# Residual additions of two attention blocks: four of nine by adding transfers, five on VectorE

## The chip, the cores and the metric

The kernel runs on one core of a Trainium2 chip. The metric is the device time of one execution in microseconds (us). Before the change it is 3370.97 us, the median of three runs (3370.32 to 3372.03). The profile is of one more execution, with a span of 3364.5 us from the first to the last instruction.

The engines are TensorE (PE in the profile, with its weight loads as PEld), VectorE (DVE), ScalarE (ACT), GpSimd (POOL) and SyncE (SP, which here only issues transfers). Each runs its own instructions in order and waits on semaphores for the others.

## The reference

The input x has 8 images of 512 channels and 32 x 32 points, in float32. Two attention blocks follow one another:

```python
def block(x, gn_w, gn_b, wq, wk, wv, bq, bk, bv, wp, bp):   # for each of two layers
    xn  = group_norm(x, 8 groups, eps=1e-5) * gn_w + gn_b     # over channels and points
    q, k, v = wq @ xn + bq, wk @ xn + bk, wv @ xn + bv        # 512 x 512 by 512 x 1024
    o   = softmax(q.T k / 8) v                                # 8 heads of 64, 1024 tokens
    return x + wp @ o + bp                                    # the residual addition
x = block(block(x, layer 0), layer 1)
```

Eight images times two layers are 16 jobs, taken in pairs of images: (image 0, layer 0), (1, 0), (0, 1), (1, 1), (2, 0) and so on. The change concerns the last line of the block, the addition of the projected output to x.

## The kernel before

Each job has three parts: a v phase, a deep phase and the attention. The v phase forms V by seven products of halves (Winograd's form of a 2 x 2 block product). The deep phase of job n forms the output O of job n - 1 and then K and Q of job n. Each of the three is again split into seven products of halves, called chains here, and each chain is split once more into seven products of 128 x 128 by 128 x 256. So the deep phase has 21 chains (O: 0 to 6, K: 7 to 13, Q: 14 to 20) with 147 products.

The products of two neighbouring chains alternate on TensorE. A chain works on four PSUM banks z, y, u, w in this order, ScalarE and VectorE taking the results out:

```python
ORDER = (1, 5, 6, 2, 7, 3, 4)            # the seven products of a chain
OUTER = (1, 2, 6, 5, 7, 3, 4)            # the seven chains of O, of K, of Q
def step(o):                             # bank that product o writes or adds into
    product(o, {1: z, 5: w, 6: z, 2: y, 7: z, 3: u, 4: z}[o], o in (1, 5))
    if o == 1:   nc.scalar.copy(y, z)
    elif o == 5: put5(w)                 # ScalarE copies w to s5
    elif o == 6: nc.scalar.copy(u, z)
    elif o == 2: put(0, 0, y)            # ScalarE: quarter of p
    elif o == 7: put(1, 1, z)            # VectorE: z + s5 into a quarter of p
    elif o == 3: put(0, 1, u)            # VectorE: u + s5
    else:        put(1, 0, z)            # ScalarE
```

The four quarters make one tile p of 128 x 1024 for each chain. All p tiles come from one pool of six buffers, so chain c writes the buffer that chain c - 6 had:

```python
LEAD = 2
epool = ctx.enter_context(tc.tile_pool(name="epool", bufs=LEAD + 4))
...
e = epool.tile([P, 2, HALF], F32, tag="e", name=f"p_{n}_{c}")
```

A p tile of O is then added into one or two quarters of x. The quarter is named by (output half, token half), and the additions are transfers, issued by GpSimd, that add to what they find:

```python
def more(oh, sh, part, ends=False):
    cols = slice(sh * HALF, (sh + 1) * HALF)
    to_ = xt[:, 2 * oh : 2 * oh + 2, cols]
    nc.gpsimd.dma_start(to_, p(part), accum_op=ALU.add)
    if ends and layer == 1:               # the last addition into this quarter
        ... later(8.0, lambda: nc.sync.dma_start(out[...], to_))

if o == 1:   more(0, 0, 1)
elif o == 2: more(0, 0, 2, True)
elif o == 6:
    add(p(6), p(6), p(1))                 # VectorE, 128 x 1024
    outer.append(lambda: more(0, 1, 6))
elif o == 5:
    more(1, 1, 5)
    outer.append(lambda: more(0, 1, 5))
elif o == 7:
    add(p(7), p(7), p(6))
    outer.append(lambda: (more(1, 1, 7, True), more(1, 0, 7)))
elif o == 3: more(0, 1, 3, True)
elif o == 4: more(1, 0, 4, True)
```

VectorE's larger work in the deep phase waits in lists, from which one piece is taken after the puts of products 7 and 3 of each chain:

```python
if ORDER[j] in (7, 3):
    if soon:  soon.popleft()()            # sums of O's inputs that a later chain needs
    if outer: outer.popleft()()           # additions of p tiles
    elif extra and extra[0][0] <= c:      # the rest: sums for K, statistics of x, ...
        extra.popleft()[1]()
```

What is left of `extra` is done in the following attention. There the normed input xn of the next job is made by ScalarE, at attention steps 22, 24, 26 and 28, with a factor mul and an offset off that VectorE computes at step 20. An attention has 64 steps.

The output bias (wp @ bv + bp) is computed once per layer from rows of wp: `multiply` forms the product with bv in place, and `add_up` sums it, for each of four row blocks.

Of the kernel before, what the change touches and what calls it, by code (L numbers as in the profile page):

```python
# [12 lines left out]
ALU = mybir.AluOpType  # L13
AX = mybir.AxisListType
# [4 lines left out]
P = 128  # L19
# [7 lines left out]
NC = C // P  # L27
# [9 lines left out]
CH = C // 2  # L37
# [33 lines left out]
def fast_path(  # L71
# [10 lines left out]
    nc = tc.nc  # L82
# [10 lines left out]
    out_bias = acts.tile([P, 2, NC], F32, name="out_bias")  # L93
# [12 lines left out]
    def later(delay, fn):  # L106
        todo.append((clock[0] + delay, fn))
# [93 lines left out]
    def used(key):  # L201
        del held[key]
        later(2.5, fetch)
# [296 lines left out]

            return [first, lambda: self.pair[1]()]

    def deep_phases(n, extra, outs=None):

# [5 lines left out]
        def job(which):  # L512
            return n - 1 if which == O else n
# [71 lines left out]
        def end(c):  # L585
            which, o = chains[c]
            m = job(which)
            used((m, which, o))

            def p(k):  # L590
                return tiles[which, k]

            def add(to_, a, b):
                outer.append(lambda: nc.vector.tensor_add(to_, a, b))  # L594

            if which == O:
                b, layer = jobs[m]
                xt = xs[b]

                def more(oh, sh, part, ends=False):  # L600

                    cols = slice(sh * HALF, (sh + 1) * HALF)
                    to_ = xt[:, 2 * oh : 2 * oh + 2, cols]
                    nc.gpsimd.dma_start(to_, p(part), accum_op=ALU.add)  # L604
                    if ends and layer == 1:
                        rows = slice(oh * CH, (oh + 1) * CH)
                        later(8.0, lambda: nc.sync.dma_start(
                            out[b, rows, cols].rearrange("(c p) s -> p c s", p=P), to_
                        ))

                if o == 1:
                    more(0, 0, 1)
                elif o == 2:
                    more(0, 0, 2, True)
                elif o == 6:
                    add(p(6), p(6), p(1))
                    outer.append(lambda: more(0, 1, 6))
                elif o == 5:
                    more(1, 1, 5)
                    outer.append(lambda: more(0, 1, 5))  # L620
                elif o == 7:
                    add(p(7), p(7), p(6))
                    outer.append(lambda: (more(1, 1, 7, True), more(1, 0, 7)))
                elif o == 3:
                    more(0, 1, 3, True)
                elif o == 4:
                    more(1, 0, 4, True)
                return
            d = dst[which]

            def quarter(oh, sh):
                return d[:, 2 * oh : 2 * oh + 2, sh * HALF : (sh + 1) * HALF]

            if o == 2:
                add(quarter(0, 0), p(1), p(2))
            elif o == 6:
                add(p(6), p(6), p(1))
            elif o == 5:
                add(quarter(0, 1), p(6), p(5))
            elif o == 7:  # L640
                add(p(7), p(7), p(6))
                add(quarter(1, 1), p(7), p(5))
            elif o == 3:
                add(quarter(0, 1), quarter(0, 1), p(3))
            elif o == 4:
                add(quarter(1, 0), p(7), p(4))

        live = {}
        soon, outer = deque(), deque()

        def thunk(c, j):
            def go():
# [21 lines left out]
        at = sorted((7 * c + 2 * j, c, j) for c in range(len(chains)) for j in range(7))  # L674
        return [thunk(c, j) for _, c, j in at]

    def plain_weights(n):
        layer = jobs[n][1]
        w = acts.tile([P, NC, C], F32, tag="deep", name="w_last")
        nc.sync.dma_start(w, wp[layer].rearrange("(cc p) o -> p cc o", p=P))  # L680
        return w
# [231 lines left out]
    def make_out_bias(layer):  # L913

        rows, bvb = [], []

        def load():
            bvb.append(apool.tile([P, C], F32, tag="px", name=f"bvb_{layer}"))
            nc.sync.dma_start(bvb[0], bv[layer : layer + 1, :].to_broadcast([P, C]))
            for i in range(2):  # L920
                rows.append(apool.tile([P, 2, HALF], F32, tag="acc", name=f"rows_{layer}_{i}"))
                nc.sync.dma_start(
                    rows[i],
                    wrows[layer][i * CH : (i + 1) * CH].rearrange("(oc p) c -> p oc c", p=P),
                )

        def multiply(oc):
            r = rows[oc // 2][:, oc % 2, :]
            nc.vector.tensor_mul(r, r, bvb[0])

        def add_up(oc):
            r = rows[oc // 2][:, oc % 2, :]
            nc.vector.tensor_reduce(out_bias[:, layer, oc : oc + 1], r, AX.X, ALU.add)
            if oc == NC - 1:
                a0 = layer * NVEC + BP
                nc.vector.tensor_add(
                    out_bias[:, layer, :], out_bias[:, layer, :], env.vec_sb[:, a0 : a0 + NC]
                )
                nc.vector.tensor_sub(
                    out_step[:, layer, :], out_bias[:, layer, 0:2], out_bias[:, layer, 2:4]  # L940
                )

        steps = [lambda oc=oc, fn=fn: fn(oc) for oc in range(NC) for fn in (multiply, add_up)]
        return load, steps

    def first_factors(put, which_layers):

# [128 lines left out]
    extra = deque((0, lambda part=part: factor(q0, part)) for part in range(4))  # L1076
    extra.append((1, lambda: store_factors(q0, 0, Q)))
    load, bias_steps = make_out_bias(0)
    extra.append((2, load))
    extra.extend((5, fn) for fn in bias_steps)  # L1080
    reads, steps = norm_steps(1)
    extra.extend((9, fn) for fn in reads)
    for n in range(-1, len(jobs)):
        last = n + 1 == len(jobs)
        outs = None
        if n >= 0:
            chores = {}

            def put(i, fn):
                while i in chores:  # L1090
                    i += 1
                chores[i] = fn

            if last:
                w = plain_weights(n)
            else:
                if n == 0:
                    first_factors(put, [(O, 0), (V, 1)])
                elif n == 1:
                    first_factors(put, [(K, 1), (Q, 1)])  # L1100
                elif n == 2:
                    first_factors(put, [(O, 1)])
                for i, (_, fn) in enumerate(extra):
                    put(2 + i, fn)
                at = (10, 20, 22, 24, 26, 28, 36, 39, 42, 45)
                for i, fn in zip(at, steps + sums(n + 1)):
                    put(i, fn)
                deep_first = deep_steps(n + 1)
                for at, fn in zip((52, 54, 57, 59), deep_first[4:]):
                    put(at, fn)  # L1110
                put(61, lambda: (extend_plan(n + 1), [fetch() for _ in range(RING)]))
            assert max(chores, default=0) < NT * len(att.groups)
            att.run(chores)
            banks(0, "one")
            banks(1, "one")
            if last:
                advance(100.0)
                advance(100.0)
                judge()
                plain_proj(n, w)  # L1120
                break
            outs = OutputSums(n)
            out_sums(n, outs)
            first = v_phase(n + 1, ORDER)
            for thunk in first[:-1]:
                thunk()
            rest = first[-1:]
            extra = deque((0, fn) for fn in deep_first[:4])
            if jobs[n][1] == 1 and jobs[n][0] + 2 < B:
                extra.append((11, lambda b=jobs[n][0] + 2: (x_tile(b), load_x(b))))  # L1130
            if n == 1:
                load, bias_steps = make_out_bias(1)
                extra.append((8, load))
                extra.extend((11, fn) for fn in bias_steps)
            if n + 2 < len(jobs):
                reads, steps = norm_steps(n + 2)
                extra.extend((15, fn) for fn in reads)
        both = deep_phases(n + 1, extra, outs)
        both[0]()
        rest[0]()  # L1140
        if n < 0:
            later(12.0, lambda: load_x(1))
        for thunk in both[1:-3]:
            thunk()
        banks(0, "two")
        att = Attention(n + 1)
        att.scores(0)
        att.scores(1)
        for thunk in both[-3:]:
            thunk()  # L1150
        banks(1, "two")
# [249 lines left out]
```

## Time and profile before

| What | Value |
|---|---|
| time, median of three runs | 3370.97 us |
| span of the profiled execution | 3364.5 us, mean granted PE clock 0.989 |
| adding transfers x<-p | 135 of 512 KB, median 8.5 us from issue to landing |
| their queue (q0) | 12.2% of 16 engines' span |
| all other transfers of the kernel (q1) | 25.0% |

Times in the profile are in microseconds from the start of the span; means of one instruction are in nanoseconds. L565 is line 565 of the kernel. Names of tiles are the program's, without numbers: `zd` is the bank z of a chain of the deep phase, `p` its tile, `x<-p` an adding transfer. In a timeline, the figures are start, duration, engine, line, operation, output and inputs, and the number of instructions merged. What stands in brackets is the time that the engine was idle before it and what ended it. TensorE executes each product of the deep phase as two records, so a row with x2 is one product. A wait for several semaphores is put down to the one that came last.

Of the lines that form the parts: L565 is a product of the deep phase, L434 of the v phase, L723 and L754 of the attention. L575 and L577 are ScalarE's puts into p, L579 and L581 VectorE's, L381 is the copy of z to y, L385 that of z to u, L594 an addition of p tiles on VectorE, and L604 the issue of an adding transfer.

### The profile page before, as it was taken

How to read it: one execution, taken by the hardware profiler on the slowest of the kernel's cores; microseconds unless marked ns; L12 is line 12 of the kernel's file. 1: busy time of each engine (PE TensorE's matmuls, PEld its weight loads, DVE VectorE, ACT ScalarE, POOL GpSimd, SP SyncE). 2: the span in 40 equal slices, each digit the busy share in tenths (PEclk: the TensorE clock that was granted, in tenths of full speed). 3: DMA queues.
4: the chain of work that ended last, by engine and by line, in shares of the span. 5: the costliest groups of instructions: out<-in, count | busy, mean ns of one | idle time of the engine just before them, and what ended most of it. 6: DMA issues, size and time to landing. Idle time of an engine off the chain costs nothing. (4 is left out here: it accounts for less than half of the span.)

```text
span 3364.5 us, 57800 instructions
## 1 busy us (share of the span) xinstructions
PE 3248.1 (97%) x22870; PEld 1872.5 (56%) x22870; DVE 2701.4 (80%) x3895; ACT 1889.1 (56%) x3022; POOL 189.3 (6%) x166
## 2 busy tenths in 40 slices
PE   9999989999999999999999999999999999999999
PEld 7365473663746638365473654736547365573743
DVE  8996978969689696886968879687796877968776
ACT  4645646456465564655646556564655646556463
POOL 0000010000100001000010000101001010010100
PEclk9999999999999999999999999999999999999999
DMA  8235271360713407135180431605417052160611
GB/s 303 92 113 135 73 222 66 99 179 21 219 33 87 120 21 181 27 99 153 30 225 24 113 89 37 174 18 132 126 42 216 15 151 57 48 160 15 164 59 40
DMA packets 169320, 351.32 MB, mean 104 GB/s; under 512 B 35033, under 2 KB 47953, under 8 KB 168017
## 3 DMA queue, kind: packets, MB, share of 16 engines
q1 hardware_dynamic: 132320, 276.77, 25.0%
q0 software_dynamic: 36720, 70.79, 12.2%
q8 instruction: 181, 2.97, 0.4%
q14 instruction: 99, 0.80, 0.1%
HBM read 224.35 MB, written 51.18 MB: 82 GB/s over the span
## 5 line engine op out<-in xcount | busy, mean ns | idle before, releaser
L728 ACT ACTIVATE e<-sc 128x1024 f32<-128x1024 f32 x1024 | 1045.3, 1023 | 585.4 <-PE sc L723 509.8
L723 PE MATMUL sc<-q,k 64*64 64x512 f32 x8192 | 1062.7, 590 | 4.5 <-ACT e L728 2.3
L754 PE MATMUL po<-e,v 64*64 64x512 f32 x8192 | 1058.1, 590 | 0.0
L740 DVE TENSOR_TENSOR acc<-acc,e 128x1024 f32<-128x1024 f32 x768 | 936.2, 1219 | 55.3 <-ACT e L728 5.6
L754 PEld LDWEIGHTS po<-e,v 64*64 64x64 f32 x8192 | 313.7, 133 | 565.5 <-issue 557.8
L723 PEld LDWEIGHTS sc<-q,k 64*64 64x64 f32 x8192 | 309.6, 133 | 565.3 <-issue 543.3
L565 PE MATMUL zd<-deep,w 128*128 128x256 f32 x892 | 264.5, 400 | 73.6 <-ACT yd L381 69.2
L604 POOL DMA_DIRECT2D x<-p x135 | 163.3, 1311 | 2114.3 <-ACT p L575 1523.4
L565 PE MATMUL vd<-deep,w 128*128 128x256 f32 x900 | 265.1, 395 | 15.4 <-ACT yd L381 11.4
L565 PEld LDWEIGHTS zd<-deep,w 128*128 128x128 f32 x892 | 174.8, 199 | 111.2 <-ACT yd L381 81.2
L738 DVE TENSOR_TENSOR acc<-e,e 128x1024 f32<-128x1024 f32 x128 | 156.3, 1221 | 92.5 <-ACT e L728 92.5
L565 PEld LDWEIGHTS vd<-deep,w 128*128 128x128 f32 x900 | 172.1, 196 | 64.4 <-ACT yd L381 16.8
L770 DVE TRANSPOSE_TENSOR_REDUCE r<-acc 128x32 f32<-128x1024 f32 x128 | 158.5, 1239 | 0.6
L579 DVE TENSOR_TENSOR p<-vd,s 128x256 f32<-128x256 f32 x63 | 26.6, 423 | 135.8 <-DMA x<-p 73.7
L565 PE MATMUL vd<-os,w 128*128 128x256 f32 x420 | 119.2, 381 | 2.0 <-DVE p L581 1.3
L594 DVE TENSOR_TENSOR p<-p,p 128x1024 f32<-128x1024 f32 x94 | 114.3, 1216 | 0.0
L434 PE MATMUL z<-w,t 128*128 128x256 f32 x480 | 111.0, 380 | 0.0
L434 PE MATMUL z<-w,xn 128*128 128x256 f32 x480 | 110.1, 383 | 0.0
L385 ACT COPY ud<-vd 128x256 f32<-128x256 f32 x173 | 61.8, 357 | 79.1 <-PE vd L565 58.1
L434 PEld LDWEIGHTS z<-w,xn 128*128 128x128 f32 x480 | 90.2, 190 | 23.6 <-issue 12.2
L447 ACT COPY v<-z 128x512 f32<-128x512 f32 x32 | 18.7, 585 | 148.7 <-PE z L434 148.7
L385 ACT COPY ud<-zd 128x256 f32<-128x256 f32 x156 | 55.7, 357 | 82.0 <-PE zd L565 81.0
(206 smaller groups left out, 4041.9 us busy)
## 6 DMA issues: line engine op xcount, KB each, us to landing
w<-deep SPq DMA_DIRECT2D x287, 448.0 KB, 4.5
x<-p POOLq DMA_DIRECT2D x135, 512.0 KB, 8.5
w<-keep SPq DMA_DIRECT2D x129, 256.0 KB, 2.7
rb<-rd SPq DMA_DIRECT2D x96, 256.0 KB, 4.0
deep<-w SPq DMA_DIRECT2D x42, 448.0 KB, 4.9
x<-x_dram SPq DMA_DIRECT2D x28, 512.0 KB, 5.4
out_dram<-x SPq DMA_DIRECT2D x28, 512.0 KB, 5.7
keep<-raw SPq DMA_DIRECT2D x5, 1792.0 KB, 7.6
```

The lines of the kernel that those rows point to most:

```text
L385: nc.scalar.copy(u, z)
L434: nc.tensor.matmul(ps[:, ti * CH : (ti + 1) * CH], r[:, cc, t0 : t0 + P], w[:, cc, :], start=(start and ti == 0 and cc == 0), stop=(cc == ...
L565: nc.tensor.matmul(ps, lhs[:, FACTOR[i], :], moving[i], start=start, stop=True, skip_group_check=True,)
L579: nc.vector.tensor_add(to_, ps, s5)
L594: outer.append(lambda: nc.vector.tensor_add(to_, a, b))
L604: nc.gpsimd.dma_start(to_, p(part), accum_op=ALU.add)
L723: nc.tensor.matmul(sc[h * HD : (h + 1) * HD, j, :], k[r, hp, k0 : k0 + HD], q[r, hp, sh * HALF : (sh + 1) * HALF], start=True, stop=True,)
L728: nc.scalar.activation(e, sc, AF.Exp, scale=SCALE)
L738: nc.vector.tensor_add(acc[g], self.es[i - 1], e)
L740: nc.vector.tensor_add(acc[g], acc[g], e)
L754: nc.tensor.matmul(po[g][j * HD : (j + 1) * HD, h, :], v[r, kc, d0 : d0 + HD], e[r, j, :], start=(kc == 0), stop=(kc == NT - 1),)
L770: nc.vector.tensor_reduce(self.r[:, 0, m, :], self.acc.pop(g).rearrange("p j (b e) -> p (j b) e", e=RP), AX.X, ALU.add, apply_transpose=True,)
```

## The change: who adds what, and in which order

Five of the nine additions of an output become VectorE instructions of 128 x 1024 elements and join the list `outer`. Four stay as transfers: parts 1 and 2 into quarter (0,0), part 3 into (0,1) and part 4 into (1,0). In jobs 0 and 2, whose weights are built on VectorE during the same chains, part 5 into (1,1) stays a transfer as well. The purpose is to have fewer transfers hold p tiles and the DMA engines. The store of a finished quarter of x is issued when the count of its additions runs out, 2 us later on the kernel's own clock where VectorE did the last, and 8 us where a transfer did.

The first four sums for K move from `extra` to `soon`, so that they do not queue behind `outer`. The factor and offset of the next job's norm move from attention step 20 to 19, three steps ahead of the first normed input. The output bias takes one instruction per row block, which multiplies and sums, and its load and steps for layer 0 are placed four chains later in the list.

```diff
-    def deep_phases(n, extra, outs=None):
+    def deep_phases(n, extra, outs=None, early=()):
...
-                def more(oh, sh, part, ends=False):
+                def more(oh, sh, part, moved=False):
                     cols = slice(sh * HALF, (sh + 1) * HALF)
                     to_ = xt[:, 2 * oh : 2 * oh + 2, cols]
-                    nc.gpsimd.dma_start(to_, p(part), accum_op=ALU.add)
-                    if ends and layer == 1:
-                        rows = slice(oh * CH, (oh + 1) * CH)
-                        later(8.0, lambda: nc.sync.dma_start(
-                            out[b, rows, cols].rearrange("(c p) s -> p c s", p=P), to_
-                        ))
+                    def go():
+                        if moved:
+                            nc.gpsimd.dma_start(to_, p(part), accum_op=ALU.add)
+                        else:
+                            nc.vector.tensor_add(to_, to_, p(part))
+                        parts[oh, sh] -= 1
+                        if layer == 1 and parts[oh, sh] == 0:
+                            rows = slice(oh * CH, (oh + 1) * CH)
+                            later(8.0 if moved else 2.0, lambda: nc.sync.dma_start(
+                                out[b, rows, cols].rearrange("(c p) s -> p c s", p=P), to_
+                            ))
+                    if moved:
+                        go()
+                    else:
+                        outer.append(go)
                 if o == 1:
-                    more(0, 0, 1)
+                    more(0, 0, 1, True)
                 elif o == 2:
                     more(0, 0, 2, True)
                 elif o == 6:
                     add(p(6), p(6), p(1))
-                    outer.append(lambda: more(0, 1, 6))
+                    more(0, 1, 6)
                 elif o == 5:
-                    more(1, 1, 5)
-                    outer.append(lambda: more(0, 1, 5))
+                    more(0, 1, 5)
+                    more(1, 1, 5, m in (0, 2))
                 elif o == 7:
                     add(p(7), p(7), p(6))
-                    outer.append(lambda: (more(1, 1, 7, True), more(1, 0, 7)))
+                    more(1, 0, 7)
+                    more(1, 1, 7)
...
-        live = {}
-        soon, outer = deque(), deque()
+        live, parts = {}, {(0, 0): 2, (0, 1): 3, (1, 1): 2, (1, 0): 2}
+        soon, outer = deque(early), deque()
...
-        def multiply(oc):
-            r = rows[oc // 2][:, oc % 2, :]
-            nc.vector.tensor_mul(r, r, bvb[0])
-
         def add_up(oc):
             r = rows[oc // 2][:, oc % 2, :]
-            nc.vector.tensor_reduce(out_bias[:, layer, oc : oc + 1], r, AX.X, ALU.add)
+            nc.vector.scalar_tensor_tensor(
+                r, r, 1.0, bvb[0], ALU.mult, ALU.mult,
+                accum_out=out_bias[:, layer, oc : oc + 1],
+            )
...
-    extra.append((2, load))
-    extra.extend((5, fn) for fn in bias_steps)
+    extra.append((6, load))
+    extra.extend((9, fn) for fn in bias_steps)
     reads, steps = norm_steps(1)
-    extra.extend((9, fn) for fn in reads)
+    extra.extend((10, fn) for fn in reads)
...
-                at = (10, 20, 22, 24, 26, 28, 36, 39, 42, 45)
+                at = (10, 19, 22, 24, 26, 28, 36, 39, 42, 45)
...
-            extra = deque((0, fn) for fn in deep_first[:4])
+            extra = deque()
...
-        both = deep_phases(n + 1, extra, outs)
+        both = deep_phases(n + 1, extra, outs, deep_first[:4] if outs else ())
```

More of the change, by code (lines that the diff above doesn't have):

```diff
@@ L941, in add_up @@
                 )
-        steps = [lambda oc=oc, fn=fn: fn(oc) for oc in range(NC) for fn in (multiply, add_up)]
-        return load, steps
+        return load, [lambda oc=oc: add_up(oc) for oc in range(NC)]
     def first_factors(put, which_layers):
```

## The prediction, made before the changed kernel ran

> **What bounds the kernel now.** I read the page's engine table first, then the busy time by stretches, the waits, and last the timeline of one stretch.
>
> ```profile
> PE 3248.1 (97%) x22870; PEld 1872.5 (56%) x22870; DVE 2701.4 (80%) x3895; ACT 1889.1 (56%) x3022; POOL 189.3 (6%) x166
> ```
>
> TensorE is busy nearly throughout, so only its pauses and its slow stretches can be won. The stretches view, cut at one attention, one v phase and one deep phase, says where they are (columns: stretch, length, then busy time and instructions of PE, PEld, DVE, ACT, POOL, then granted clock, DMA share, GB/s):
>
> ```profile
> 1773.30:1881.70 108.40, 108.40 (x1010) 38.60 (x1009) 98.16 (x114) 71.22 (x74) 1.42 (x1) 1.00 0.08 19
> 1881.70:1906.30 24.60, 24.60 (x114) 21.72 (x115) 22.97 (x44) 6.07 (x11) 0.00 (x0) 1.00 0.35 113
> 1906.30:1979.80 73.50, 68.30 (x310) 56.63 (x309) 44.49 (x75) 41.46 (x106) 10.87 (x9) 0.98 0.73 180
> ```
>
> Attention and v phase have no gap on PE. The deep phase has, and a slowed clock, while VectorE is busy for 44.49 of 73.50 us. Its floor: 147 products, one of which starts ahead of the stretch; neighbours start 0.4317 us apart in the timeline, so 146 x 0.4317 = 63.0 us, and two score steps of 0.86 us make 64.75 us. The same cut for all fifteen deep phases behind an attention gives 76.6, 81.8, 78.6, 78.2, 73.0, 74.1, 75.7, 75.7, 73.5, 73.4, 75.1, 74.2, 74.9, 74.5 and 73.0 us, in sum 1132.3. The floors are 15 x 64.75 = 971, so **161 us** of the run lie above the floor, all in these phases.
>
> ```profile
> ACT p L575 <- DMA x<-p: 71.6, 26, 5.5
> PE zd L565 <- ACT yd L381: 69.2, 29, 4.5
> ACT p L577 <- DMA x<-p: 67.3, 25, 4.8
> ...
> PE vd L565 <- DMA w<-deep: 8.5, 6, 2.3
> ```
>
> These are waits of the whole run (total us, times, longest). PE waits for a ScalarE copy, and ScalarE waits for the adding transfers. The timeline of the first pause in the stretch above joins them:
>
> ```profile
> 1936.09 0.59 PE L565 MATMUL ud<-t,w 128*128 128x256 f32 x2
> 1938.83 0.37 ACT L575 COPY p<-yd 128x256 f32<-128x256 f32 x1 [3.80 <-DMA x<-p]
> 1938.86 0.42 DVE L579 TENSOR_TENSOR p<-vd,s 128x256 f32<-128x256 f32 x1 [4.67 <-DMA x<-p]
> 1939.10 0.38 ACT L381 COPY yd<-zd 128x256 f32<-128x256 f32 x1
> ...
> 1939.53 0.97 PE L565 MATMUL zd<-deep,w 128*128 128x256 f32 x2 [2.85 <-ACT yd L381]
> ```
>
> A new product tile p takes a buffer that a transfer into x still reads. ScalarE cannot write it, the next bank copy is stuck behind it in the in-order queue, and PE stops for 2.85 us. Then each product takes about 0.85 us instead of 0.43 for some four products: 1.8 us more. VectorE is held in the same way, so its idle time there is no sign of a light load.
>
> [...]
>
> **The change part by part.**
>
> *Five additions off the transfers.* The page counts 135 transfers x<-p, nine for each of fifteen outputs, median 8.5 us to landing. Four stay (62 in all, with one more in each of two outputs). Do these still block? In the stretch at 1906 the second transfer starts at 1917.5 and must land before chain 7 writes p: its first put is product 52 of the stretch, 1906.3 + 51 x 0.4317 = 1928.3. Even with 9.7 us, the middle of the transfers around it, it lands at 1927.2. The third and fourth leave at about 1925 and 1929 and have until 1940 and 1943. Tiles 5, 6 and 7 are free once VectorE has added them, by about 1930 where chain 8 needs the first at 1931.8. So the pauses for x<-p should be **gone**, and the half-rate stretches with them. Transfers also get room: the q0 row's 12.2% of 16 engines over 3364.5 us, divided by 135, is 3.0 us of all engines each; five fewer free 15 us per phase.
>
> *The same five on VectorE.* 73 additions x 1.216 = 89 us in the run, about 6.1 per phase. In sum they fit: 44.5 + 6.1 = 50.6 of some 67 us. But they stand in a row where VectorE is already tight. Its order in the stretch before:
>
> ```profile
> 1921.12 0.42 DVE L579 TENSOR_TENSOR p<-vd,s 128x256 f32<-128x256 f32 x1
> 1921.61 0.42 DVE L579 TENSOR_TENSOR p<-ud,s 128x256 f32<-128x256 f32 x1
> 1923.77 0.48 DVE L581 SCALAR_TENSOR_TENSOR p<-vd,out_step,s 128x256 f32<-128x256 f32 x1 [1.74 <-PE vd L565]
> 1924.17 1.22 DVE L594 TENSOR_TENSOR p<-p,p 128x1024 f32<-128x1024 f32 x1
> 1925.31 0.48 DVE L581 SCALAR_TENSOR_TENSOR p<-ud,out_step,s 128x256 f32<-128x256 f32 x1
> 1926.80 0.48 DVE L581 SCALAR_TENSOR_TENSOR p<-zd,out_bias,s 128x256 f32<-128x256 f32 x1 [1.01 <-PE zd L565]
> 1927.66 0.48 DVE L581 SCALAR_TENSOR_TENSOR p<-ud,out_bias,s 128x256 f32<-128x256 f32 x1 [0.38 <-PE ud L565]
> ```
>
> In the new program one addition stands ahead of the first of these lines, one behind it, one behind the second, one behind the fifth and one behind the sixth. Start to start an addition takes 1.14 us, a put 0.34 or 0.40. The chain's last product writes the bank that the put of product 7 reads: it follows by four products, 1.73 us, and the put starts 0.64 us after product 7 starts and takes 0.42, so the put may be late by some 0.55 us before PE waits. Chain 4: ready at 1920.75, now begun at 1922.26, 1.51 late, so PE waits 0.95. Chain 5: ready at 1924.72 with that shift, begun at 1925.22: 0.50 late, no wait to speak of. Chain 6: ready 1927.75, begun 1928.30: 0.55, at most 0.1. Chain 7 is on time. So the additions give back about **1.05 us per phase**, in pauses too short to slow the clock (in the same stretch a 1.21 us pause cost nothing after it).
>
> *An ordinary phase after:* 64.75 + 1.15 (the last chain runs alone, and its score steps begin: read from start-to-start gaps at 1975 to 1980, unchanged) + 1.05 = 67.0 us. Five of the twelve windows from the fourth on carry w<-deep waits beside loads of x; I leave 0.5 us each. Sum 12 x 67.0 + 2.5 = 806 against 895.3.
>
> *The first three* build weights on VectorE as well, four steps of 0.93 us together per chain. Windows 1 and 3 lose 2.5 us in the early chains now; with the extra additions and a wait of (1,1) for its moved transfer I put them at 71 and 71.5. Window 2 builds K and Q weights behind the additions: 72.5. Sum 215 against 237.0.
>
> *Offsets earlier:* in the first and third attentions, 109.8 and 110.4 us against 108.4, ScalarE waited for off 1.8 and 2.4 us and PE behind it. One step, 1.7 us, earlier removes it: 3.4 us.
>
> *Output bias:* eight passes of 0.68 us become four of about 0.7, twice; in the first pass the 3.3 us pause came from a weight load (w<-keep), which this does not touch, and the loads stand at the same place in SyncE's order. I count 0.
>
> Sum: 89 + 22 + 3.4 = 114.5 us, less 5 for small waits not seen: 3371 - 110 = **3261 us**.
>
> **The rivals.** (a) *VectorE becomes the bound of the output part.* For it: over chains 3 to 5 it has 4.6 (two pairs of output sums lie there too), 3.0 and 3.1 us of work per 3.02 us of PE. Against: it catches up in chain 6. If each chain lost as chain 4 does, 3 us more per phase: 3305. (b) *The remaining transfers still block,* because the weights asked for earlier slow them: DMA share 0.71 to 0.90 in these phases speaks for it, the 15 us freed against. One pause with its slow clock, 4 us, in each: 3320. (c) *Weights become the wait* as the phase gets shorter: 8.5 us now, in six phases whose x loads sit in one queue behind stores of x that wait for transfers. The last transfer should land some 10 us earlier, more than the phase gains by then. If wrong, 1 to 2 us per phase: 3280. (d) *Everything vanishes,* with the puts in time: 3245.
>
> **Range and chances.** The pauses before are surely of the transfers' making, and the order on PE and ScalarE is unchanged; the width comes from (a) and (c), about 1.5 us for each of fifteen phases. 3238 to 3292. Within 2% means above 3303.6, which takes (b), or (a) in full: 4%. Slower needs both and more.
>
> **What would show it.** Waits of ACT p and DVE p for x<-p near zero; PE zd <- ACT yd under 10 us; a wait of PE for DVE p of about 1 us at the fifth chain in every phase; deep stretches of 66 to 68 us with clock 1.00; 62 transfers; attention 108.4 everywhere. It is wrong if PE waits for VectorE repeat over several chains, or w<-deep grows.

## The result, and the profile after

The changed kernel takes **3247.6 us** (median of four runs, 3243.87 to 3248.85) against 3370.64 us for four runs of the kernel before: ratio **0.963**, 95% interval 0.962 to 0.965. That is 123 us less. The prediction was 3261 us, with 3238 to 3292 as its range.

From the page after: the engine table, the row of the queue of adding transfers (packets, MB, share of 16 engines) and the row of these transfers (number, size, median us to landing):

```profile
PE 3203.7 (99%) x22870; PEld 1846.3 (57%) x22870; DVE 2771.0 (85%) x3968; ACT 1896.9 (59%) x3022; POOL 98.9 (3%) x93
...
q0 software_dynamic: 16864, 32.51, 6.2%
...
x<-p POOLq DMA_DIRECT2D x62, 512.0 KB, 6.9
```

VectorE got 73 instructions and 70 us more and the run is shorter. PE's busy time fell by 44.4 us though it does the same products. Most of that is half-rate time that has gone: the mean granted clock was 0.989 before and is 1.0 after, and 0.011 of 3364.5 us is 37 us. The span shrank by 122.5 us, from 3364.5 to 3242.0; the other 78 us are pauses. Half as many transfers land sooner, 6.9 us in the median.

The stretches view after, cut as before at one attention, the v phase behind it and the deep phase:

```profile
1701.30:1809.70 108.40, 108.40 (x1009) 38.45 (x1008) 98.05 (x114) 71.31 (x74) 1.42 (x1) 1.00 0.08 19
1809.70:1834.40 24.70, 24.70 (x118) 21.75 (x115) 23.10 (x44) 6.07 (x11) 0.00 (x0) 1.00 0.35 112
1834.40:1901.30 66.90, 65.83 (x309) 55.44 (x308) 49.67 (x80) 42.03 (x106) 4.80 (x4) 1.00 0.59 159
```

Attention and v phase are what they were. The deep phase went from 73.50 to 66.90 us with a full clock. VectorE's own work in it rose by 5.2 us, from 44.49 to 49.67. The fifteen deep phases after are 70.2, 73.0, 69.2 and then twelve of 66.9 us (a cut to tenths shows 66.8 for four of them), in sum 1015.2 where it was 1132.3. So **117.1 of the 122.5 us** come from there. The first and third attention gave 3.4 us, the pass ahead of the first attention 2.1.

The waits of PE after, whole run (total us, times, longest); the two left out, 1.5 us each, are at lines outside the deep phase's products:

```profile
PE vd L565 <- DVE p L579: 12.6, 15, 1.6
PE vd L565 <- DVE p L581: 6.7, 22, 0.7
PE zd L565 <- DVE p L579: 4.5, 4, 2.9
PE v L434 <- DVE q L790: 2.5, 1, 2.5
...
PE zd L565 <- DVE p L581: 0.9, 2, 0.7
```

The 69.2 us for ScalarE's copy yd are gone and so are the 8.5 us for w<-deep. No put into p, on either engine, waits for a transfer any more. One new wait has come: the first line, fifteen times. PE's timeline shows it at the same place in each of the twelve ordinary phases (start, duration, engine, instruction, idle before it):

```profile
1849.55 0.59 PE L565 MATMUL vd<-os,w 128*128 128x256 f32 x2
1850.87 0.70 PE L565 MATMUL vd<-os,w 128*128 128x256 f32 x2 [0.72 <-DVE p L579]
1851.40 0.59 PE L565 MATMUL yd<-q,w 128*128 128x256 f32 x2
```

and VectorE's timeline says why (L467 and L468 are sums of O's inputs, L610 an addition to x):

```profile
1848.59 0.41 DVE L467 TENSOR_TENSOR os<-to 128x256 f32<-128x256 f32 x1
1848.93 0.41 DVE L468 TENSOR_TENSOR os<-to,os 128x256 f32<-128x256 f32 x1
1849.26 1.22 DVE L610 TENSOR_TENSOR x<-x,p 128x1024 f32<-128x1024 f32 x1
1850.40 0.41 DVE L579 TENSOR_TENSOR p<-vd,s 128x256 f32<-128x256 f32 x1
```

The put of product 7 of chain 4 (L579, last line) stands behind an addition to x that needed no haste: the run with it one place later, below, loses nothing by it. VectorE has no idle time in these lines: the put is late because of what is ahead of it, not because its bank was.

### The profile page after: what moved, and what is told of

Same layout as the page of the kernel before. It is cut to its first block, busy times and chain, and to the rows that moved or that the text cites. A ratio compares the mean times of both kernels' runs of the same rounds, so it can differ in the third digit from the quotient of the medians.

```text
span 3242.0 us, 57681 instructions
## 1 busy us (share of the span) xinstructions
PE 3203.7 (99%) x22870; PEld 1846.3 (57%) x22870; DVE 2771.0 (85%) x3968; ACT 1896.9 (59%) x3022; POOL 98.9 (3%) x93
## 3 DMA queue, kind: packets, MB, share of 16 engines
q0 software_dynamic: 16864, 32.51, 6.2%
## 4 chain that ended last, share of the span: by engine, by line
PE 89%; DVE 8%; DMA 1%; issue 1%; ACT 0%; DVEq 0%; SPq 0%
PE sc L736 26%; PE po L767 26%; PE vd L565 10%; PE zd L565 9%; PE z L434 6%; PE yd L565 4%; PE ud L565 3%; PE v L434 1%; PE u L434 1%; PE y L434 1%; DVE acc L753 1%; PE pp L705 1%; DVE p L581 1%; DVE x L610 1%; DVE p L594 1%
## 5 line engine op out<-in xcount | busy, mean ns | idle before, releaser
L741 ACT ACTIVATE e<-sc 128x1024 f32<-128x1024 f32 x1024 | 1046.8, 1024 | 584.9 <-PE sc L736 499.3
L565 PE MATMUL vd<-deep,w 128*128 128x256 f32 x900 | 256.3, 383 | 5.1 <-DVE p L581 4.9
L565 PE MATMUL zd<-deep,w 128*128 128x256 f32 x892 | 248.1, 380 | 3.8 <-DVE p L579 3.2
L608 POOL DMA_DIRECT2D x<-p x62 | 74.6, 1203 | 1996.8 <-ACT p L575 1521.9
L583 ACT COPY s<-zd 128x256 f32<-128x256 f32 x173 | 64.5, 373 | 71.5 <-PE zd L565 71.5
L434 PEld LDWEIGHTS z<-w,xn 128*128 128x128 f32 x480 | 90.0, 190 | 23.8 <-issue 12.2
```

The source lines that it names most:

```text
L434: nc.tensor.matmul(ps[:, ti * CH : (ti + 1) * CH], r[:, cc, t0 : t0 + P], w[:, cc, :], start=(start and ti == 0 and cc == 0), stop=(cc == ...
L565: nc.tensor.matmul(ps, lhs[:, FACTOR[i], :], moving[i], start=start, stop=True, skip_group_check=True,)
L583: return chain(product, lambda ps: nc.scalar.copy(s5, ps), put, z, y, u, w)
L741: nc.scalar.activation(e, sc, AF.Exp, scale=SCALE)
```

## The experiments

Two theories were to be told apart. **Landing:** adding transfers land after the moment at which their p tile is wanted again; with five fewer they land in time. **Holding:** what counts is how many tiles are held by transfers at all, whatever else is on the queues. The expectations of the first four runs (the additions alone, the bytes put back on the same queue, and the two with a smaller ring) set holding against **load**, the theory that the traffic as such slows the phase. Landing is how the prediction argued, with a time of landing and a limit for each transfer; as a theory for these runs it was named only after those four. Beside that: what the five additions cost VectorE, and whether that must be paid.

### The additions alone

The kernel after, with the offset again at attention step 20 and the output bias in two passes at its old place:

```diff
-                at = (10, 19, 22, 24, 26, 28, 36, 39, 42, 45)
+                at = (10, 20, 22, 24, 26, 28, 36, 39, 42, 45)
+        def multiply(oc): ...            # and tensor_reduce in add_up, as before
```

> The changed kernel with the offsets back at step 20 and the output bias as before: the additions alone. Holding theory: the deep phases keep their gain of 117 us, the attentions lose 3.4 us and the first pass 2.1: 3253 us, 3249 to 3257. Rival (the small parts do more than counted): above 3262.

Measured: 3250.05 us (four runs), ratio 0.965, interval 0.964 to 0.967. The ordinary deep phases are again 66.9 us. The other two parts of the change move 2 to 7 us, by which runs of the whole change it is set against, and this many runs do not give that more closely. All else is the additions, together with the first four sums for K, which stay in `soon` here.

### The same nine transfers, one eighth of the bytes

The kernel before, with each adding transfer on 64 of 512 columns. It leaves out seven eighths of the residual additions; the order and number of the transfers, and what they must wait for, are those of before:

```diff
-                    nc.gpsimd.dma_start(to_, p(part), accum_op=ALU.add)
+                    nc.gpsimd.dma_start(to_[:, :, : HALF // 8], p(part)[:, :, : HALF // 8], accum_op=ALU.add)
```

> The kernel before, all nine additions as transfers in the same order and with the same waits, but each on an eighth of its columns (64 of 512), so that seven eighths of the additions are left out. Theory (how long a transfer takes to land decides): landings of 3 to 4 us, no waits for x<-p, no VectorE additions: deep phases of 65.9 to 66.6 us as with the five additions left out, 3232 to 3240 us. Rival (the row of nine issues with their waits for one another on GpSimd is what holds the tiles): most of the pauses stay, above 3300.

Measured: 3229.36 us, ratio 0.958 (0.957 to 0.960), a little under what was expected. Still 135 transfers hold their tiles and the buffers are six, yet the puts wait for x<-p once in the whole run:

```profile
ACT p L577 <- DMA x<-p: 0.7, 1, 0.7
```

The instructions of the adding transfers in one deep phase give the reason (last row of that view: us to landing, shortest, median, longest). First the kernel before, phase at 1906:

```profile
L604 POOL DMA_DIRECT2D x<-p x9: 1200/1200/1706, 1911.1 to 1945.4; - x9
...
DMA to landing us min/median/max: 5.9/8.3/13.6
```

then the one with thin transfers, the same phase:

```profile
L604 POOL DMA_DIRECT2D x<-p x9: 1200/1200/2212, 1832.7 to 1855.1; - x9
...
DMA to landing us min/median/max: 2.8/4.6/5.5
```

So the number of held tiles is not it: nine are held in both, but for less time in the second. GpSimd's own waits for an earlier x<-p fell over the whole run from 160.0 us (36 times) to 66.7 us (15 times). The run leaves open whether it is a transfer's own bytes or the load of all nine on the DMA engines that makes them land late; their queue fell from 12.2% of 16 engines to 3.4%. The stretches view of this phase gives a clean size for a deep phase, with no pause but 0.2 us at its end:

```profile
1827.90:1893.80 65.90, 65.55 (x311) 55.65 (x309) 44.41 (x75) 42.00 (x106) 10.92 (x9) 1.00 0.52 138
```

65.90 us is the prediction's floor of 64.75 plus 1.15. Fifteen such phases would be 988.5 us, 143.8 less than before. The first three, which build weights, are longer here too (68.7, 68.4 and 68.4 us), so that the trace's own fifteen gain 136 us. The run is 140.6 us shorter than its neighbour runs of the kernel before (3369.91).

### The bytes put back, on the same queue

The kernel after, with a transfer of 1 MB from SBUF to a spare place in DRAM beside each of the 73 additions on VectorE, issued by GpSimd like the adding ones:

```diff
+        nc.gpsimd.dma_start(spare[turn[0] % 10], deep_x[0][:, :, 2:4, :])
...
                             nc.vector.tensor_add(to_, to_, p(part))
+                            copy_out()
```

> The changed kernel, and beside each of its VectorE additions a transfer of 1 MB from SBUF to a place in DRAM that nothing reads. By the q0 and q1 rows of before (3.0 us of all engines for an adding transfer of 512 KB, about 1.6 us for a plain one) this puts back as much DMA time as the five transfers took, but it holds no p tile. Holding theory: 3248 to 3265 us, ACT p waits for x<-p under 20 us. Load theory: most of the gain is lost again, 3320 to 3370.

Measured: 3374.26 us, ratio 1.002 (1.001 to 1.003). **The whole gain is gone**, with 62 held tiles. That is against what I had written; the theory of holding falls in this form. The time lies just above what load named, 3320 to 3370, but it is the p tiles through which the load acts. Their waits (whole run) are back. With eight lines inserted, L585 and L589 are the puts L577 and L581 of before, L573 the products, L389 the copy yd:

```profile
DVE p L589 <- DMA x<-p: 58.7, 12, 5.8
PE vd L573 <- ACT yd L389: 58.5, 24, 4.5
ACT p L585 <- DMA x<-p: 53.0, 13, 5.5
```

The adding transfers of its phase at 1908:

```profile
L616 POOL DMA_DIRECT2D x<-p x4: 1192/1203/1216, 1912.8 to 1932.5; - x4
...
DMA to landing us min/median/max: 5.7/12.3/20.8
```

and those of the kernel after, phase at 1834:

```profile
L608 POOL DMA_DIRECT2D x<-p x4: 1200/1200/1200, 1839.2 to 1858.9; - x4
...
DMA to landing us min/median/max: 5.9/6.8/8.0
```

The four leave at the same time in both, 4.8 us after the start of the phase the first and 24.5 us the last. Only the landing differs, and only that of the third and fourth. GpSimd's timeline in the phase with the copies (L149) shows what lay ahead of the third:

```profile
1920.31 3.51 POOL L149 DMA_DIRECT2D spare<-deep  x4
1929.48 1.21 POOL L616 DMA_DIRECT2D x<-p  x1 [5.67 <-ACT yd L389]
1930.25 1.22 POOL L149 DMA_DIRECT2D spare<-deep  x1
1932.54 1.19 POOL L616 DMA_DIRECT2D x<-p  x1 [1.06 <-ACT yd L389]
```

Four copies of 1 MB, then the third adding transfer, which lands 17.7 us after its issue, where it took 5.9 without copies; then a fifth copy and the fourth transfer, 20.8 us where it took 8.0.

### The same bytes on another queue

The same with the copies issued by ScalarE, which has a queue of its own (76.55 MB on it, and 32.51 MB on GpSimd's):

```diff
-        nc.gpsimd.dma_start(spare[turn[0] % 10], deep_x[0][:, :, 2:4, :])
+        nc.scalar.dma_start(spare[turn[0] % 10], deep_x[0][:, :, 2:4, :])
```

> The run with 1 MB transfers again, but issued by ScalarE, on a queue of their own and no longer ahead of the adding transfers on GpSimd's. In the run before, the third adding transfer of a phase stood behind four of them and held its p tile past its limit. Theory (a p tile is held until its transfer lands, and what stands ahead in the same queue decides when): landings of x<-p near 7 to 10 us, ACT p waits for x<-p under 20 us, 3248 to 3280 us, what is lost being waits for w<-deep. Rival (the DMA engines as such are the limit, whatever the queue): landings above 11 us again and 3330 to 3380.

Measured: 3340.04 us, ratio 0.992 (0.990 to 0.993). The time fits the rival, and so does the median landing over the whole run, 11.7 us; the waits of the puts fit the theory. In the corresponding phase the landings are

```profile
DMA to landing us min/median/max: 6.0/10.7/12.7
```

so that the longest is 12.7 us instead of 20.8, but also instead of the 8.0 without copies. The median over the whole run is no better than the 11.3 us with the copies on GpSimd's queue, as in an ordinary phase the second transfer lands later here and the last two sooner. The DMA engines carry as much in both runs (GpSimd's queue 11.8% of 16 engines there, 5.7% and 6.3% for the two queues here). So traffic on another queue delays an adding transfer too, and traffic ahead of it on its own queue delays the last two more. The puts wait 9.9 us for x<-p in the whole run instead of 177. The largest wait of PE is new here, that for ScalarE's copy ud (L393):

```profile
PE zd L573 <- ACT ud L393: 47.7, 14, 7.6
```

Its cause stands in ScalarE's own timeline:

```profile
1914.92 4.11 ACTq L149 DMA_DIRECT2D spare<-deep  x1
1915.08 0.48 ACT L585 ACTIVATE p<-yd,out_bias 128x256 f32<-128x256 f32 x1
1915.44 0.39 ACT L389 COPY yd<-zd 128x256 f32<-128x256 f32 x1
1919.07 0.37 ACT L591 COPY s<-vd 128x256 f32<-128x256 f32 x1 [3.24 <-PE vd L573]
```

Issuing one copy takes 4.11 us, and the copy L591, which comes after it, starts only when it has ended, as the times show. The bracket names PE, but the times show the issue as what ended last. The last two landings are longer behind 1 MB copies on the same queue (17.7 and 20.8 us) than beside such copies on another (11.5 and 12.7 us); by what mechanism, these runs do not show. Yet a held ScalarE also delays the puts themselves (the one behind L591 starts only at 1919.64), so that tiles are wanted later. With the issue times of the kernel after, landings of 12.7 us would put the fourth transfer at 37.2 us into the phase, by estimate, where the prediction's limit was 36.7. So the few waits for x<-p do not show that such traffic on another queue is harmless. That was not tried with an issuer that is not held.

### The number of buffers

The kernel before had no room for a seventh p tile, so two deep-phase weight buffers were given up; a control gives up the weights alone:

```diff
-RING = 7
+RING = 5
-    epool = ctx.enter_context(tc.tile_pool(name="epool", bufs=LEAD + 4))   # second kernel only
+    epool = ctx.enter_context(tc.tile_pool(name="epool", bufs=LEAD + 5))
```

> Control for the next run: the kernel before with a ring of five weight buffers in place of seven (the room that a seventh p buffer needs). Both theories: no faster than before; 3371 to 3410 us, with the wait of PE for w<-deep above the 8.5 us of before.

> The kernel before with seven p buffers (and the ring of five), all nine additions still transfers, the traffic the same. Holding theory (a p tile that a transfer still reads blocks the next tile in its buffer): each tile has one chain, 3.0 us, more to be read; the last of the nine transfers still lands late, so some 3 us per phase are won and not 8: 30 to 60 us below the control, waits of ACT p for x<-p about half. Load theory (the transfers' traffic is what slows the deep phase): within 5 us of the control.

Measured: control 3422.17 us, ratio 1.016 (1.014 to 1.018), 12 us above what was expected of it; with seven p tiles 3415.11 us, ratio 1.015 (1.013 to 1.016). The seventh tile brought 7 us where 30 to 60 were expected, and the intervals overlap. The puts' waits for x<-p fell from 122 to 80 us, but they were 291 in the kernel before. It says little, because the control had a new bound (a wait of the seven-tile kernel; the control has 69.3 us of it):

```profile
PE vd L565 <- DMA w<-deep: 70.2, 20, 5.8
```

The other way round was better to read: the kernel after with only five p buffers.

```diff
-    epool = ctx.enter_context(tc.tile_pool(name="epool", bufs=LEAD + 4))
+    epool = ctx.enter_context(tc.tile_pool(name="epool", bufs=LEAD + 3))
```

> The changed kernel with five p buffers in place of six, so that each tile must be free one chain, 3.0 us, earlier. Theory with the landing times of the changed kernel's trace (phase at 1834.4: landings at about 1845.8, 1853.4, 1861.8 and 1867, limits with five buffers 1851, 1854, 1866 and 1870): still no wait, 3246 to 3252 us. Rival (six buffers are needed for the tiles of O, as their number is what bounds the phase): waits for x<-p return, 3270 to 3330.

Measured: 3252.33 us (3247.66 to 3253.22), ratio 0.965 (0.963 to 0.966): at most some 5 us above the kernel after. Waits of the puts for x<-p come back, little of them; the larger is

```profile
ACT p L577 <- DMA x<-p: 8.4, 6, 2.9
```

The expectation of no wait at all was missed by a little. So with four transfers that land in 6 to 8 us in an ordinary phase, one buffer fewer is nearly free; with nine that take up to 13.6 us in the phase shown, six were too few.

### What the additions cost VectorE

The five additions left out, so that x gets only the four parts by transfer:

```diff
-                            nc.vector.tensor_add(to_, to_, p(part))
+                            pass
```

> The changed kernel with the five VectorE additions left out, so that x gets only the four parts that the transfers add: it shows what the additions on VectorE cost. Theory: the pauses of PE for DVE p go, about 1.0 us per phase, 3230 to 3236 us. Rival (the additions lie wholly beside other work): 3245 to 3248; rival (they cost more than the pauses show): below 3225.

Measured: 3229.77 us, ratio 0.959 (0.957 to 0.961). The unchanged kernel after was run again in the same comparison, as its control:

> The changed kernel once more, as the control for the next run on the same chip: ratio to before 0.963 to 0.965.

It took 3247.46 us (ratio 0.965, 0.963 to 0.966). Against it the additions cost 17.7 us, or 1.2 per phase, while the 73 of them keep VectorE busy for 88.5 us in the trace of the kernel after (1213 ns each in the mean). Without the additions the deep phase is 65.90 us again:

```profile
1825.30:1891.20 65.90, 65.55 (x309) 55.65 (x308) 44.38 (x75) 42.03 (x106) 4.80 (x4) 1.00 0.60 161
```

Then all nine on VectorE, with no adding transfer at all:

```diff
-                    more(0, 0, 1, True)       # and so for parts 2, 3, 4 and 5
+                    more(0, 0, 1)
```

> The changed kernel with all nine additions on VectorE, no adding transfer at all. If VectorE is near its limit in the output chains (four more additions of 1.14 us there): pauses of 1 to 2 us in several chains, 2 to 4 us more per phase, 3275 to 3310 us. If VectorE still has room: no pause beyond the 0.72 us, 3245 to 3255.

Measured: 3268.31 us, ratio 0.971 (0.970 to 0.973): between the two expectations, 21 us above the kernel after, still some 100 below the one before. Its deep phase:

```profile
1847.30:1915.60 68.30, 66.36 (x309) 55.20 (x308) 53.97 (x84) 42.00 (x106) 0.00 (x0) 1.00 0.40 125
```

VectorE does 53.97 us of work in 68.30 us and PE waits for a put of product 7 at two places, 0.39 and 1.17 us. Its sum leaves room, so these waits look like a matter of order too; for nine additions that is not shown, for five the next run tests it.

### One place later in the list

If the pause at chain 4 comes from the order, an empty entry in the list should remove it: each later addition to x is taken one place later.

```diff
                     add(p(6), p(6), p(1))
+                    outer.append(lambda: None)
                     more(0, 1, 6)
```

> The changed kernel with one empty piece in VectorE's list after the addition of p(6) and p(1), so that the five additions to x each come one slot later (half a chain). The put of chain 4 then stands 0.4 us late and no longer 1.5. Theory (the put of chain 4 waits behind the first addition): the 0.72 us pause in each phase goes, and the deep phase falls from 66.9 to about 66.0 us; 15 phases, 10 to 15 us, 3233 to 3238 us. Rival (the additions as such are too much for VectorE in these chains, wherever they stand): the pause moves to chain 5 or 6 and the time stays at 3247.

Measured: **3235.44 us** (3234.52 to 3236.25), ratio 0.961 (0.960 to 0.962), as expected, 12 us under the kernel after. Of the fifteen waits in the first line of PE's waits above one is left:

```profile
PE vd L565 <- DVE p L579: 0.5, 1, 0.5
```

The ordinary phase has the same work and no pause at chain 4:

```profile
1831.80:1897.70 65.90, 65.55 (x309) 55.65 (x308) 49.60 (x80) 42.00 (x106) 4.80 (x4) 1.00 0.59 161
```

The additions are free in this phase: 49.60 us of VectorE in the length that 44.38 us had. Over the run they still cost some 6 us against the kernel without them, at intervals that overlap. The first deep phase became 2.8 us longer, as VectorE stood still for the moved part 5:

```profile
252.62 1.23 DVE L610 TENSOR_TENSOR x<-x,p 128x1024 f32<-128x1024 f32 x1 [3.89 <-DMA x<-p]
```

The addition of part 7 to the same quarter must wait until the transfer of part 5 has landed. So in the last kernel job 0 adds part 5 on VectorE as well; only job 2 keeps the exception:

```diff
-                    more(1, 1, 5, m in (0, 2))
+                    more(1, 1, 5, m == 2)
```

> The kernel with the additions one slot later, and part 5 of job 0 on VectorE too, so that the exception holds for job 2 alone. In the first output phase VectorE stood still 3.9 us for the moved transfer into (1,1). Theory: that wait goes and an addition of 1.14 us comes, the first phase gets 2 to 4 us shorter, the others stay: 3231 to 3234 us. Rival (VectorE is full in that phase because it builds weights, which is why the exception is there): the phase gets no shorter, 3235 to 3238.

Measured: 3233.29 us (3232.45 to 3233.60), ratio 0.959 (0.958 to 0.961). The wait of 3.89 us is gone and the first phase is 5 us shorter; the phases around it give most of that back. It is the fastest complete kernel here, 2 us ahead of the one before it at intervals that overlap.

## Why the prediction was right, step by step

**The bound and its cause: right.** The pauses of the deep phase came from p tiles that late transfers held. The thin transfers show it most directly, as nine tiles are still held, each for less time: 140.6 us, where the excess over a phase of 65.9 us was 143.8 in all. And bytes ahead in the queue bring the loss back at the same four issue times.

**Four transfers land in time: right, with room.** Worked out were landings at 20.9 us into the phase for the second against a limit of 22.0; measured is 19.0. I put 9.7 us for its landing, the middle of the transfers around it; it took 7.6, and the same transfer had taken 7.5 in the kernel before. The third and fourth landed at 27.4 and 32.5 us, their limits being 33.7 and 36.7.

**The additions give back 1.05 us per phase: right in sum, not in all its places.** Measured against the phase without them, 66.9 - 65.9 = 1.0 in an ordinary phase, and 1.2 from times over all. The wait is at chain 4 alone. By the lines above, PE's product comes 1.32 us behind the one before it where 0.43 is usual, so it is 0.89 us late where 0.95 was worked out (0.72 of it is shown as idle), and the next comes 0.10 us late on top. Chain 6, for which I allowed 0.1, has none. That these deviations nearly cancel is luck.

**The ordinary phase, 67.0: right** (66.8 to 66.9). The 2.5 us left for w<-deep waits were too much: there is no such wait.

**The first three, 215: 212.4, a little under.** The first and third were shorter than I put them (70.2 and 69.2 for 71 and 71.5), the second a little longer (73.0 for 72.5). The wait of quarter (1,1) for its moved transfer is there once, 2.1 us.

**Offsets, 3.4: right.** The first and third attention are 108.5 and 108.3 us; with the offset at step 20 again, in the run with the additions alone, they are 109.8 and 110.5.

**Output bias, 0: here was a miss of 2.1 us.** The pause for the weight load stays, but at 2.89 us instead of 3.32, and four products at half rate behind it, 4 x 0.43 = 1.7 us, are gone. This second part does not belong to the change: in the repeated run of the same kernel the pause was 2.77 us and the half rate was there. So these 1.7 us are luck of the profiled execution.

Where the 13 us between 3261 and 3247.6 lie: 5 taken off the gain for small waits not seen, which did not come; 2.5 for weights; 2.6 in the first three phases; 2.1 in the first pass; 1.2 in the twelve ordinary ones. Nearly every term was put on the slow side. (The parts of the gain, 89, 22 and 3.4, add to 114.4 and not 114.5.)

**The rivals.** (a) VectorE as the bound: at one chain only, and the run with all nine there shows a second. (b) Remaining transfers block: no; with traffic put ahead of them they do, so it was a fair rival. (c) Weights: no. (d) Everything vanishes: no in this kernel, yes in an ordinary phase one place later. By the time alone (d), at 3245, is nearer than 3261; only the 0.72 us pause in each phase tells them apart. Where the pauses did vanish, the time was 3235.44, so that 3245 was too slow for (d) as well.

## What to carry to other kernels

When an engine waits to write a buffer that a transfer reads, compare the time of landing with the time at which the buffer is wanted again, and count what is queued ahead of the transfer (behind four copies of 1 MB the third adding transfer landed after 17.7 us, without them after 5.9); here fewer bytes (landings of 4.6 us in the median for 8.3 in one phase) took the pauses away without a buffer more. Moving work onto a busy engine cost time here (0.72 us of idle TensorE in an ordinary phase) where it landed ahead of something that was waited for, so after moving it, look for that place and shift the work by one. A version that keeps the order and number of the transfers and takes their bytes away tells held buffers from late landings in one run.

## What was not expected of the hardware

**A slowed TensorE does not follow from the length of a pause alone.** In the pass ahead of the first attention eleven of the profiles here, the one before among them, have a pause of 2.4 to 3.7 us at the same place. Half-rate products followed it after 2.36, 2.42, 2.77, 3.20, 3.32, 3.45 and 3.65 us, and did not after 2.60, 2.66, 2.89 and 3.13 us. The kernel after and its repetition differ in this: 2.89 us with no slow product and 2.77 us with a mean clock of 0.81 over the 9 us from 67. Two lines of PE from the run with the additions alone, behind its pause of 3.20 us, show such products at 0.86 us from start to start:

```profile
69.19 1.06 PE L565 MATMUL vd<-t,w 128*128 128x256 f32 x2
70.05 1.06 PE L565 MATMUL vd<-deep,w 128*128 128x256 f32 x2
```

So 2.36 us was enough in one run and 3.13 us was not in another. What decides it is not shown.

**Issuing a transfer can hold ScalarE.** Of the 73 issues of a 1 MB copy half took 0.52 us, and the longest 4.7. What makes one of them long is not shown.

**Sum and product in one instruction cost one small extra.** The bias step is 0.68 us and a read of the accumulator of 0.08 us, where two passes took 0.68 us each.
